# Group-norm statistics on ScalarE in place of VectorE, and one more product with C on VectorE in a quarter of layer 0's steps

## The chip, the cores and the metric

The kernel runs on one core of a Trainium2 chip. The metric is the device time of one execution in microseconds (us). The engines are called as the profile calls them: PE (TensorE, matmul), DVE (VectorE), ACT (ScalarE), POOL (GpSimd) and SP (SyncE, which issues all DMAs here). Each works through its own queue in order.

## What is computed

The input x is (8, 384, 32, 32) in float32: 8 batches, 384 channels, 1024 tokens. Four layers follow each other, each of the form x = x + f(gn(x)), where gn is a group norm over 32 groups of 12 channels and all 1024 tokens.

```python
def _gn(v, G=32, eps=1e-5):
    g = v.reshape(B_, G, C_ // G, H_, W_)
    m = jnp.mean(g, axis=(2, 3, 4), keepdims=True)
    s = jnp.var(g, axis=(2, 3, 4), keepdims=True)
    return ((g - m) / jnp.sqrt(s + eps)).reshape(v.shape)
...
def step(h, inp):                       # layers 0 and 2, over 1024 tokens
    dt_t, B_t, C_t, u_t = inp
    dA = jnp.exp(dt_t[..., None] * A)
    h = dA * h + (dt_t * u_t)[..., None] * B_t[:, None, :]
    y = jnp.einsum('bdn,bn->bd', h, C_t)
    return (h, y)
```

Layers 0 and 2 are Mamba blocks: a projection to 2 x 768 channels, a causal convolution of width 3, silu, a projection to dt, B and C, the recurrence above with 16 states for each of 768 channels, a gate silu(z), and a projection back to 384. Layer 2 has a layer norm ahead of it and an MLP (384 to 1536 to 384, gelu) behind. Layer 1 is a 1x1 projection, a filter in the Fourier domain of 8x8 patches, a depthwise 3x3 convolution, a gelu gate and a 1x1 projection. Layer 3 is a depthwise 3x3 convolution.

## The kernel before

**Tiling.** Each batch is cut into two chunks of T = 512 tokens. Layer 0 works through 16 chunks (numbers 0 to 15), layer 2 through 16 more (16 to 31). Layer 1 of a batch runs beside the later chunks of layer 0, layer 3 beside those of layer 2. Layer 1's result goes to HBM (x_mid) and comes back for layer 2.

**A step.** The recurrence of a chunk takes NQ = 24 steps. A step i has 32 channels x 16 states, held as four tiles of 128 partitions x 512 tokens, j = 0 to 3. For each step:
- begins: a DMA spreads dt*u from HBM into a tile g of 128 x 4 x 512 (5 buffers).
- times: POOL multiplies all of g by B (bc[:, 0], 2048 columns).
- decays: PE spreads dt into the four PSUM banks dA0 to dA3 (one buffer each).
- exps: ACT makes exp(A*dt) in place in each bank.
- scans: DVE runs the recurrence, tile by tile. For j below `low` the result goes into g, for the others into the bank dA.
- carries: in a batch's first chunk ACT copies the last column as the next chunk's start.
- states: POOL multiplies the tiles below `low` in g by C (bc[:, 1]).
- The other tiles are multiplied by C on DVE, out of the bank into g, right after the four scans.
- gathers: PE sums over the states into y; gatings: DVE multiplies y by the gate.

`low` is 4 minus the step's entry in SHARE. Before, every step has share 2: two tiles are multiplied by C on POOL in one operation of 1024 columns, two on DVE in two operations of 512. A decay for the next step waits until the bank's last reader is done: the scan for j below `low`, the product for the others.

**Statistics.** group_stats collects the mean and variance of each channel row (3 blocks of 512 columns for each of two halves), then two small matmuls with gmat average over the group. It is called once for each batch and layer, 32 times. For batches of layer 0 after the first, and for layer 2, `measure` loads 128 x 512 blocks from HBM through two xk buffers; for the first batch, layer 1 and layer 3 the blocks are already in SBUF. Before, each block is one bn_stats on DVE, and bn_aggr joins the six.

**Order.** The order of instructions on each queue is written by a planner when the kernel is built. Every piece of work is a generator; `yield on("ACT", ...)` names the engine of its next instruction and its operands. `Order.run` takes, again and again, the piece that could begin soonest by a table of costs (class Clocks), with the recurrence's processes first. Work beside the recurrence is spread by `pace`, and three PSUM banks (NBANK) are handed out by ps_take and ps_give. start_jobs adds the jobs of a chunk when its first step begins.

Of the kernel before, what the change touches and what calls it, by code (L numbers as in the profile page):

```python
# [9 lines left out]
F32 = mybir.dt.float32  # L10
# [6 lines left out]
P = 128  # L17
# [29 lines left out]
NBANK = 3  # L47
LEAD = 2
PATIENCE = 6.0
TAPS, LAST_TAPS = 4, 4  # L50
SHARE = (2, 2, 2, 2)
SET_EXP = "natural_log_exp_and_others"


# [195 lines left out]
def tile_conv_preact_d4(ctx: ExitStack, tc: tile.TileContext, a: dict, out: bass.AP):  # L250
# [179 lines left out]


    def group_stats(blocks, read=None):
        st = new(wk, [P, 2 * KC, 6], F32, "st", 2)
        mv = new(wk, [P, 2], F32, "mv", 2)
        for h, k, v, then in blocks():
            yield on("DVE", v)
            vector.bn_stats(st[:, h * KC + k, :], v)
            if then:
                yield from then()
        if read:  # L440
            read()
        yield on("DVE", st)
        vector.bn_aggr(mv, _flat(st))
        nmean, spread, rstd, nbias = (
            new(wk, [P, 1], F32, tag, 4) for tag in ("gnm", "gsp", "grstd", "gnb")
        )
        yield on("PE", mv, when=bank)
        ps, tag = ps_take("ps_gn")
        mm(ps[:, 0:1], gmat, mv[:, 0:1])
        yield on("ACT", ps)  # L450
        act(nmean, ps[:, 0:1], AF.Copy, scale=-1.0)
        ps_give(ps, tag)
        act(spread, mv[:, 0:1], AF.Square, bias=nmean)
        act(spread, spread, AF.Identity, bias=mv[:, 1:2])
        yield on("PE", spread, when=bank)
        ps, tag = ps_take("ps_gn")
        mm(ps[:, 0:1], gmat, spread)
        yield on("ACT", ps)
        rsqrt(rstd, ps[:, 0:1], eps_gn)
        ps_give(ps, tag)  # L460
        act(nbias, nmean, AF.Identity, scale=rstd)
        return rstd, nbias
# [2 lines left out]
        rstd, nbias = stats  # L465
        act(dst, src, AF.Identity, scale=rstd, bias=nbias)

    def measure_first():
        def blocks():
            for h in range(NCH):  # L470
                for k in range(KC):
                    yield h, k, first[h][:, k, :], None

        chunks[0]["stats"] = yield from group_stats(blocks)

    def measure(s):
        yield on(None, when=xk_free.when)
        xk_free.take()

        def load(h, k):  # L480
            x = new(wk, [P, T], F32, "xk", 2)
            sync.dma_start(x, _rows(s["src"][s["b"], :, h * T : (h + 1) * T])[:, k, :])
            return x

        places = [(h, k) for h in range(2) for k in range(KC)]
        loaded = []
        for h, k in places[:2]:
            yield on("SP")
            loaded.append(load(h, k))

        def blocks():
            for q, (h, k) in enumerate(places):

                def then():
                    if q + 2 < len(places):
                        yield on("SP")
                        loaded.append(load(*places[q + 2]))

                yield h, k, loaded[q], then

        s["stats"] = yield from group_stats(blocks, xk_free.give)

# [91 lines left out]
    def front(s):  # L594
# [23 lines left out]

        def block(d):
            if n not in (0, B * NCH - 1, B * NCH):  # L620
                yield pace(s["t"] - 18 + d)
            ps, tag = yield from projection(s, "ps_in", d * P)
            yield on("ACT", ps)
            act(u[d], ps, AF.Identity, scale=vec[:, d, 2:3], bias=vec[:, d, 3:4])
            if c < NCH - 1:
                act(s["xt"][:, d, :], ps[:, T - 2 : T], AF.Copy)
            for j in (1, 2):
                yield on("DVE", u[d])
                vector.scalar_tensor_tensor(
                    u[d][:, j:T], ps[:, 0 : T - j], vec[:, d, 2 - j : 3 - j],  # L630
                    u[d][:, j:T], ALU.mult, ALU.add,
                )
            ps_give(ps, tag)
# [35 lines left out]

        def step(d):  # L670
            if n not in (0, B * NCH - 1, B * NCH):
                yield pace(s["t"] - 9 + 3 * d)
# [12 lines left out]
            yield on("DVE", m, when=dt_free.when)  # L685
            dt_free.take()
            v = new(wk, [P, T], F32, "dt", 2)
            vector.scalar_tensor_tensor(v, ps, 0.0, m, ALU.max, ALU.add)
            ps_give(ps, tag)
            yield on("ACT", v, when=pc_free.when)  # L690
            pc_free.take()
            pc = new(wk, [P, NPC, T], BF16, "pc", 2)
            act(pc[:, 0, :], v, AF.Copy)
            if s["pre"] == "l0_":
                yield on("PE", pc[:, 0, :], when=bank)
                rest, tag = ps_take("ps_dr")
                mm(rest, eye, v, stop=False)
                mm(rest, minus, pc[:, 0, :], start=False)
                m_free.give()
            else:  # L700
                yield on("POOL", pc[:, 0, :])
                gpsimd.tensor_sub(m, v, pc[:, 0, :])
                rest, tag = m, None
            order.add(scaled(d, v), s["t"] - 14)
            yield on("ACT", rest)
            act(pc[:, 1, :], rest, AF.Copy)
            if tag:
                yield on("DVE", pc[:, 1, :])
# [32 lines left out]
    def seen(*keys):  # L741
# [4 lines left out]

        return ready

    def begins():
        for t, (s, i) in enumerate(steps):  # L750
            k, sub = QUADS[i]
# [30 lines left out]
    def decays():  # L782
        for t, (s, i) in enumerate(steps):
            k, sub = QUADS[i]
            for j in range(4):
                procs["decays"]["due"] = t - 2
                yield on("PE", when=lambda: (
                    None if ("begin", t) not in said or t > 0 and (
                        ("scan" if j < 4 - SHARE[(i - 1) % NSUB] else "product", t - 1, j) not in said
                        or j > 0 and not carried(t - 1, j)  # L790
                    )
                    else max(clocks.known(s["dts"][k]), clocks.last.get(dAs[j].name, 0.0))
                ))
                mm(dAs[j], selr[:, j, :], s["dts"][k][:, sub, :])
                said["decay", t, j] = True
# [9 lines left out]
    def scans():  # L805
        for t, (s, i) in enumerate(steps):
            for j in range(4):
# [2 lines left out]
                    else clocks.known(s["g", i][:, j, :])  # L810
                ))
                g = s["g", i]
                low = 4 - SHARE[i % NSUB]
                q = 4 * i + j
                vector.tensor_tensor_scan(
                    g[:, j, :] if j < low else dAs[j],
# [14 lines left out]
    def carries():  # L831
        for t, (s, i) in enumerate(steps):
            if s["c"] == NCH - 1:
                continue
            low = 4 - SHARE[i % NSUB]
# [11 lines left out]

    def carried(t, j):
        s, i = steps[t]
        low = 4 - SHARE[i % NSUB]  # L850
        return s["c"] == NCH - 1 or ("carry", t, j) in said or 0 < j < low

    def states():
        for t, (s, i) in enumerate(steps):
            low = 4 - SHARE[i % NSUB]
# [168 lines left out]
    def layer1(s):  # L1024
# [4 lines left out]
        def blocks():  # L1029
            for h in range(2):  # L1030
                for k in range(KC):
                    yield h, k, x[h][:, k, :], None

        gn = yield from group_stats(blocks)
        hurry = s["n"] == B * NCH - 1
        for hb in range(H // PS):
            if not hurry:
# [181 lines left out]
    def layer3(s):  # L1219
# [4 lines left out]
        def blocks():  # L1224
            for h in range(2):
                for k in range(KC):
                    yield h, k, x[h][:, k, :], None

        gn = yield from group_stats(blocks)
        taken = [0]  # L1230
        taps = TAPS if b < B - 1 else LAST_TAPS
        for k in range(KC):
# [47 lines left out]
    def start_jobs(t):  # L1280
# [2 lines left out]
            return  # L1283
        s = chunks[n]
        order.add(gates(s, 1), t + 8)
        if s["c"] == 0 and n + NCH < len(chunks):
            m = chunks[n + NCH]
            order.add(measured(m), t + NQ + 4)
        if n + 1 < len(chunks):
            later = chunks[n + 1]  # L1290
            order.add(front(later), t + NQ - 26)
# [177 lines left out]
```

## Time and profile before

| | |
|---|---|
| median of 3 runs | 6279.72 us (6264.88 to 6286.1) |
| the profiled execution, its own time | 6281.34 us |
| its span, first to last instruction | 6279.6 us |
| busy: PE, DVE, ACT, POOL | 5835.6, 5623.6, 4234.9, 5720.2 us |
| granted TensorE clock, mean | 0.965 |
| HBM traffic | 190 GB/s over the span |

A line of a group reads: source line, engine, operation, output tile <- input tiles, shapes, count, then busy time in us and mean ns of one, then the idle time of the engine just before and what ended it. Nearly all instructions carry line 189, that of a helper, so groups are told apart by tile names. A line of waits reads: who waited <- for whom: us in total, times, longest. In a table of stretches, each engine has its busy us and its count of instructions. PE's ends are modelled, so a busy PE is not PE at its peak.

### The profile page before, as it was taken

To read this page: it belongs to the slowest core of one execution; us is meant where nothing else is said; L and a number is where in the kernel's file an instruction comes from. 1 tells how busy PE (TensorE), PEld (TensorE's weight loads), DVE (VectorE), ACT (ScalarE), POOL (GpSimd) and SP (SyncE) were. 2 spreads that over 40 slices of the span, in tenths; PEclk is the share of its full clock that TensorE was granted. 3 is DMA by queue.
4 is the path that set the end of the run, shared out by engine and by line. 5 is a ranking of instruction groups with operands and counts; after the bars stand their busy time and mean duration, and the time that the engine had idled before them with its cause. 6 is when DMAs were issued, how large, how long until landed. Compare 5 with 4: busy or idle time off the path is not lost.

```text
span 6279.6 us, 62636 instructions
## 1 busy us (share of the span) xinstructions
PE 5835.6 (93%) x19010; PEld 2196.0 (35%) x19010; DVE 5623.6 (90%) x6392; ACT 4234.9 (67%) x7940; POOL 5720.2 (91%) x2022
## 2 busy tenths in 40 slices
PE   6878999999999999989989999999999999999997
PEld 2223333333333333333333333333333333333333
DVE  4999989999999989988887999999998999989992
ACT  4656677677767667766676766777677676667752
POOL 4999989999998999989997999999999999999980
PEclk8889999999999999999999999999999999999998
DMA  6877878887887878877777888888787787887871
GB/s 174 189 186 185 193 186 194 206 189 192 195 191 182 193 197 199 200 183 179 185 178 182 203 205 208 213 201 209 191 214 195 196 208 189 207 203 197 197 186 35
DMA packets 345860, 1195.88 MB, mean 190 GB/s; under 512 B 40420, under 2 KB 142484, under 8 KB 247220
## 3 DMA queue, kind: packets, MB, share of 16 engines
q1 hardware_dynamic: 345524, 1191.88, 78.0%
q8 instruction: 152, 2.49, 0.2%
q14 instruction: 184, 1.51, 0.1%
HBM read 1040.73 MB, written 150.99 MB: 190 GB/s over the span
## 4 chain that ended last, share of the span: by engine, by line
DVE 18%; PE 14%; POOL 12%; ACT 7%; issue 5%; DMA 3%; SPq 0%; DVEq 0%; POOLq 0%; ACTq 0%
POOL g L189 10%; DVE g L189 8%; DVE dA L189 5%; PE ps_up L189 3%; PE ps_dn L189 2%; PE y L189 2%; DMA g<-dud 2%; DVE ps_dw L189 2%; ACT dA L189 2%; PE dA L189 2%; DVE u L189 1%; PE ps_dw L189 1%; ACT h L189 1%; ACT L370 1%; ACT L189 1%
## 5 line engine op out<-in xcount | busy, mean ns | idle before, releaser
L189 POOL TENSOR_TENSOR g<-g,bc 128x1024 f32<-128x1024 f32 (+1 forms) x1536 | 5241.0, 3445 | 279.4 <-ACT carry L189 111.8
L189 ACT ACTIVATE dA<-dA,w_A 128x512 f32<-128x512 f32 x3072 | 2018.6, 661 | 964.1 <-PE dA L189 952.5
L189 PE MATMUL dA<-dts,selr 96*128 96x512 bf16 x3072 | 1193.7, 391 | 248.1 <-DVE g L189 223.7
L189 DVE TENSOR_TENSOR_SCAN g<-dA,carry,g 128x512 f32<-128x512 f32 x768 | 954.7, 1270 | 70.8 <-POOL g L189 55.2
L189 DVE TENSOR_TENSOR g<-dA,bc 128x512 f32<-128x512 f32 x1536 | 994.5, 678 | 20.4 <-ACT carry L189 18.8
L189 DVE TENSOR_TENSOR_SCAN dA<-dA,carry,g 128x512 f32<-128x512 f32 x768 | 953.8, 1273 | 42.6 <-ACT dA L189 42.1
L189 DVE TENSOR_TENSOR_SCAN dA<-dA,g 128x512 f32<-128x512 f32 x768 | 910.2, 1212 | 65.8 <-ACT dA L189 65.5
L189 DVE TENSOR_TENSOR_SCAN g<-dA,g 128x512 f32<-128x512 f32 x768 | 908.0, 1209 | 61.8 <-POOL g L189 43.9
L189 PE MATMUL y<-g,sely 128*32 128x512 f32 x6144 | 866.9, 632 | 47.0 <-POOL g L189 44.4
L189 PEld LDWEIGHTS <-selr 96*128 96x128 bf16 x3072 | 300.8, 99 | 1117.6 <-issue 1070.2
L189 PE MATMUL ps_in<-xf,w_in 128*128 128x512 f32 x1152 | 574.0, 619 | 3.7 <-ACT xf L189 3.3
L189 PE MATMUL ps_dn<-h,mw 128*128 128x512 f32 x1152 | 556.5, 605 | 13.9 <-ACT h L189 8.0
L189 PE MATMUL ps_z<-xf,w_in 128*128 128x512 f32 x1152 | 564.3, 596 | 4.0 <-DVE dt L189 3.6
L189 PE MATMUL ps_up<-t,mw 128*128 128x512 f32 x1152 | 556.9, 597 | 5.0 <-DVE acc L189 1.8
L189 PE MATMUL ps_out<-u,w_out 128*128 128x512 f32 x1152 | 552.0, 595 | 0.2 <-DVE x L189 0.2
L189 PE MATMUL ps_dw<-tp,diag 128*128 128x512 f32 x864 | 435.0, 606 | 8.9 <-ACT diag L189 8.8
L189 PEld LDWEIGHTS y<-g,sely 128*32 128x32 f32 x6144 | 127.6, 109 | 618.4 <-issue 296.1
L189 PEld LDWEIGHTS ps_dn<-h,mw 128*128 128x128 f32 x1152 | 218.8, 193 | 288.1 <-issue 245.5
L189 PEld LDWEIGHTS ps_in<-xf,w_in 128*128 128x128 f32 x1152 | 220.8, 197 | 273.8 <-issue 237.0
L189 POOL TENSOR_TENSOR dt<-dt,u 128x512 f32<-128x512 f32 x192 | 244.1, 1273 | 74.6 <-ACT pc L189 60.0
L189 PEld LDWEIGHTS ps_up<-t,mw 128*128 128x128 f32 x1152 | 215.6, 191 | 265.6 <-issue 227.5
L189 PEld LDWEIGHTS ps_z<-xf,w_in 128*128 128x128 f32 x1152 | 215.9, 190 | 253.2 <-issue 219.6
(112 smaller groups left out, 6471.2 us busy)
## 6 DMA issues: line engine op xcount, KB each, us to landing
g<-dud SPq DMA_DIRECT2D x768, 1024.0 KB, 7.8
dtd<-pc SPq DMA_DIRECT2D x192, 384.0 KB, 3.9
dts<-dtd SPq DMA_DIRECT2D x192, 384.0 KB, 7.8
mw<-in_l_mlp_w SPq DMA_DIRECT2D x192, 384.0 KB, 6.1
dud<-dt SPq DMA_DIRECT2D x768, 64.0 KB, 3.2
xf<-in_x SPq DMA_DIRECT2D x16, 768.0 KB, 9.2
x<-in_x SPq DMA_DIRECT2D x16, 768.0 KB, 11.4
x_mid<-x SPq DMA_DIRECT2D x16, 768.0 KB, 7.4
```

The source lines that it names most:

```text
L189: return call(out_, *args, **kw)
L370: nc.scalar.preload_act_table_set(SET_EXP)
```

## The change

There are three parts.

1. group_stats works on ACT in place of DVE. Each block is copied onto itself with a running sum along its columns (accum_out), and squared, less a shift, with another running sum. The shift is minus the mean of the first block, so that the squares stay small. Blocks loaded from HBM (junk is False) are squared in place. Chunks in SBUF are copied as one operation of 1536 columns, and squared in three of 512 into a PSUM bank whose content is not used. Five small ACT operations at the end give mean and variance.
2. SHARE is given for each layer. In layer 0 one step of four has share 3: one tile is multiplied by C on POOL, three on DVE. Layer 2 keeps share 2.
3. In layer 0 the statistics of a batch are asked for one chunk earlier, at the start of a batch's second chunk, three chunks ahead. In layer 2 they stay where they were. The small tiles of statistics get 6 buffers in place of 4.

```diff
-SHARE = (2, 2, 2, 2)
+SHARE = {"l0_": (2, 3, 2, 2), "l2_": (2, 2, 2, 2)}
...
     def group_stats(blocks, read=None):
-        st = new(wk, [P, 2 * KC, 6], F32, "st", 2)
-        mv = new(wk, [P, 2], F32, "mv", 2)
-        for h, k, v, then in blocks():
-            yield on("DVE", v)
-            vector.bn_stats(st[:, h * KC + k, :], v)
+        st = new(wk, [P, 2, 2 * KC], F32, "st", 2)
+        mv = new(wk, [P, 5], F32, "mv", 2)
+        shift, mean, off, sq, var = (mv[:, q : q + 1] for q in range(5))
+        count = 0
+        for v, junk, then in blocks():
+            columns = v.free_size()
+            yield on("ACT", v)
+            act(v, v, AF.Copy, accum_out=st[:, 0, count : count + 1])
+            if count == 0:
+                act(shift, st[:, 0, 0:1], AF.Copy, scale=-1.0 / columns)
+            if junk:
+                yield on("ACT", when=bank)
+                ps, tag = ps_take("ps_sq")
+                for k in range(KC):
+                    act(ps, v[:, k, :], AF.Square, bias=shift, accum_out=st[:, 1, KC * count + k : KC * count + k + 1])
+                ps_give(ps, tag)
+            else:
+                act(v, v, AF.Square, bias=shift, accum_out=st[:, 1, count : count + 1])
+            count += 1
             if then:
                 yield from then()
         if read:
             read()
-        yield on("DVE", st)
-        vector.bn_aggr(mv, _flat(st))
+        yield on("ACT", st)
+        act(st[:, 0, 0:count], st[:, 0, 0:count], AF.Copy, scale=1.0 / L / KC, accum_out=mean)
+        act(st[:, 1, :], st[:, 1, :], AF.Copy, scale=1.0 / L / KC, accum_out=var)
+        act(off, shift, AF.Identity, bias=mean)
+        act(sq, off, AF.Square)
+        act(var, sq, AF.Identity, scale=-1.0, bias=var)
...
-        yield on("PE", mv, when=bank)
+        yield on("PE", mean, when=bank)
         ps, tag = ps_take("ps_gn")
-        mm(ps[:, 0:1], gmat, mv[:, 0:1])
+        mm(ps[:, 0:1], gmat, mean)
...
-                yield h, k, loaded[q], then
+                yield loaded[q], False, then
...
+    def share(t):
+        s, i = steps[t]
+        return SHARE[s["pre"]][i % NSUB]
...
                 g = s["g", i]
-                low = 4 - SHARE[i % NSUB]
+                low = 4 - share(t)
...
-        gn = yield from group_stats(blocks)
+        gn = yield from group_stats(whole_chunks(x))
...
-        if s["c"] == 0 and n + NCH < len(chunks):
-            m = chunks[n + NCH]
-            order.add(measured(m), t + NQ + 4)
+        ahead_by = NCH + 1 if s["c"] == 1 and n + NCH < B * NCH else NCH
+        for m in chunks[n + NCH : n + NCH + 2]:
+            if m["c"] == 0 and "asked" not in m and m["n"] - n <= ahead_by:
+                m["asked"] = True
+                order.add(measured(m), t + NQ + 4)
```

The new whole_chunks yields x[0] and x[1], each whole, with junk set to True; measure_first, layer1 and layer3 use it. In scans, carries, carried, states and decays the step's share is read through share(t).

More of the change, by code (lines that the diff above doesn't have):

```diff
@@ L49 @@
 PATIENCE = 6.0
-TAPS, LAST_TAPS = 4, 4
-SHARE = (2, 2, 2, 2)
+TAPS, LAST_TAPS = 4,4
+SHARE = {"l0_": (2, 3, 2, 2), "l2_": (2, 2, 2, 2)}
 SET_EXP = "natural_log_exp_and_others"
@@ L441, in group_stats @@
             read()
-        yield on("DVE", st)
-        vector.bn_aggr(mv, _flat(st))
+        yield on("ACT", st)
[4 more added lines that the diff above has]
+        act(var, sq, AF.Identity, scale=-1.0, bias=var)
         nmean, spread, rstd, nbias = (
-            new(wk, [P, 1], F32, tag, 4) for tag in ("gnm", "gsp", "grstd", "gnb")
+            new(wk, [P, 1], F32, tag, 6) for tag in ("gnm", "gsp", "grstd", "gnb")
         )
-        yield on("PE", mv, when=bank)
+        yield on("PE", mean, when=bank)
         ps, tag = ps_take("ps_gn")
-        mm(ps[:, 0:1], gmat, mv[:, 0:1])
+        mm(ps[:, 0:1], gmat, mean)
         yield on("ACT", ps)
@@ L452, in group_stats @@
         ps_give(ps, tag)
-        act(spread, mv[:, 0:1], AF.Square, bias=nmean)
-        act(spread, spread, AF.Identity, bias=mv[:, 1:2])
+        act(spread, mean, AF.Square, bias=nmean)
+        act(spread, spread, AF.Identity, bias=var)
         yield on("PE", spread, when=bank)
@@ L466, in group_norm, with whole_chunks, measure_first @@
         act(dst, src, AF.Identity, scale=rstd, bias=nbias)
-    def measure_first():
+    def whole_chunks(x):
         def blocks():
             for h in range(NCH):
-                for k in range(KC):
-                    yield h, k, first[h][:, k, :], None
-        chunks[0]["stats"] = yield from group_stats(blocks)
+                yield x[h], True, None
+        return blocks
+    def measure_first():
+        chunks[0]["stats"] = yield from group_stats(whole_chunks(first))
     def measure(s):
@@ L620, in block @@
             if n not in (0, B * NCH - 1, B * NCH):
-                yield pace(s["t"] - 18 + d)
+                yield pace(s["t"] + -18 + 1 * d)
             ps, tag = yield from projection(s, "ps_in", d * P)
@@ L671, in step @@
             if n not in (0, B * NCH - 1, B * NCH):
-                yield pace(s["t"] - 9 + 3 * d)
+                yield pace(s["t"] + -9 + 3 * d)
             ps, tag = yield from chain(
@@ L788, in decays @@
                     None if ("begin", t) not in said or t > 0 and (
-                        ("scan" if j < 4 - SHARE[(i - 1) % NSUB] else "product", t - 1, j) not in said
+                        ("scan" if j < 4 - share(t - 1) else "product", t - 1, j) not in said
                         or j > 0 and not carried(t - 1, j)
@@ L834, in carries @@
                 continue
-            low = 4 - SHARE[i % NSUB]
+            low = 4 - share(t)
             yield on("ACT", when=lambda: (
@@ L849, in carried @@
         s, i = steps[t]
-        low = 4 - SHARE[i % NSUB]
+        low = 4 - share(t)
         return s["c"] == NCH - 1 or ("carry", t, j) in said or 0 < j < low
@@ L854, in states @@
         for t, (s, i) in enumerate(steps):
-            low = 4 - SHARE[i % NSUB]
+            low = 4 - share(t)
             procs["states"]["due"] = t + 0.3
@@ L1027, in layer1 @@
         yield once(lambda: "layer1" in said and (s["n"] < NCH or "done" in chunks[s["n"] - NCH]))
[L1029 to L1032, printed above, removed]
-        gn = yield from group_stats(blocks)
+        gn = yield from group_stats(whole_chunks(x))
         hurry = s["n"] == B * NCH - 1
@@ L1222, in layer3 @@
         yield once(lambda: s["n"] < (B + 1) * NCH or "done" in chunks[s["n"] - NCH])
[L1224 to L1229, printed above, removed]
+        gn = yield from group_stats(whole_chunks(x))
         taken = [0]
```

## Prediction

> **What bounds the kernel now.** I read the busy row of each engine first, then the same by stage, then the groups by shape, then who waits for whom.
>
> ```profile
> PE 5835.6 (93%) x19010; PEld 2196.0 (35%) x19010; DVE 5623.6 (90%) x6392; ACT 4234.9 (67%) x7940; POOL 5720.2 (91%) x2022
> 700.00:2500.00 1800.00, 1694.65 (x5798) 640.12 (x5797) 1686.32 (x1918) 1265.07 (x2527) 1721.83 (x575) 0.97 0.80 193
> 3200.00:5600.00 2400.00, 2317.23 (x7436) 876.02 (x7429) 2201.38 (x2486) 1684.86 (x2973) 2265.75 (x842) 0.99 0.81 200
> ```
>
> The two lower lines are the stages (columns: length, then busy of PE, weight loads, DVE, ACT, POOL). The first is steady layer 0 with layer 1 beside it, the second steady layer 2 with layer 3. Three engines are nearly level in both; only ACT has room (70%). POOL does 480 operations on g in the first stretch and 587 in the second, 48 to a chunk: 10.0 chunks of 180.0 us, and 12.2 of 196 us. Per chunk of layer 0 that is POOL 172.2 us (95.7%), PE 169.5 (94.2%), DVE 168.6 (93.7%), ACT 126.5 (70.3%); of layer 2, PE 189.5 (96.6%), POOL 185.3 (94.4%), DVE 180.0 (91.7%), ACT 137.8 (70.2%). So POOL is fullest in layer 0, and PE in layer 2.
>
> The groups by shape give the prices:
>
> ```profile
> L189 POOL TENSOR_TENSOR g<-g,bc 128x2048 f32<-128x2048 f32 x768 | 3478.2, 4533 | 107.9 <-DMA g<-dud 98.8 <-PE dA L189 2.3 <-PE ps_dt L189 2.0
> L189 POOL TENSOR_TENSOR g<-g,bc 128x1024 f32<-128x1024 f32 x768 | 1808.9, 2357 | 171.5 <-ACT carry L189 111.8 <-DVE g L189 57.9 <-PE dA L189 0.3
> L189 DVE TENSOR_TENSOR g<-dA,bc 128x512 f32<-128x512 f32 x1536 | 994.5, 678 | 20.4 <-ACT carry L189 18.8
> L189 DVE BATCH_NORM_STATS2 st<-xk 128x6 f32<-128x512 f32 x90 | 60.8, 676 | 0.2 <-DMA xk<-x_mid 0.2
> L189 DVE BATCH_NORM_AGGREGATE mv<-st 128x2 f32<-128x36 f32 x32 | 9.6, 300 | 0.1
> L189 ACT ACTIVATE u<-u 128x1536 f32<-128x1536 f32 x64 | 91.5, 1476 | 0.4
> L189 ACT ACTIVATE sq<-xf 128x512 f32<-128x512 f32 x48 | 30.0, 625 | 13.8 <-DVE xf L189 13.8
> L189 ACT ACTIVATE gsp<-mv,gnm 128x1 f32<-128x1 f32 x32 | 9.4, 295 | 1.2 <-ACT gnm L189 0.2
> ```
>
> See that a statistic on DVE costs what a product with C costs there (676 and 678 ns), so the two can be exchanged one for one; and that POOL's 1024-wide product waits most for ACT's carry copies.
>
> The waits of steady layer 0, DVE's and then POOL's:
>
> ```profile
> DVE u L189 <- PE y L189: 36.5, 28, 2.6
> DVE dA L189 <- ACT dA L189: 21.5, 17, 2.4
> DVE x L189 <- PE ps_out L189: 18.4, 5, 3.9
> ...
> POOL g L189 <- ACT carry L189: 33.5, 16, 4.1
> POOL g L189 <- DMA g<-dud: 30.5, 13, 5.1
> ```
>
> DVE's largest wait is for y, which PE can gather only after POOL's product: POOL holds DVE up there. The next on both engines is for ACT, the engine that is to get the new work.
>
> **What the Trainium skill says.** "ScalarE: Activation LUTs", section "What ACT_TABLE_LOAD costs": each pointer operand adds about 93 ns to an ACTIVATE. The trace agrees: h<-ps_up with one pointer takes 687 ns, t<-ps_out without one 595. "Perfetto Trace Analysis", section "Identifying the Most-Contended Engine", says that matmul busy time is no measure of distance to PE's limit; this trace shows 94% in layer 0 and 96.6% in layer 2 on that row, so PE's row has at least that much left in layer 0. "GPSIMD Engine Reference", section "Elementwise — side-by-side cycle accounting", has 4497 ns for a 2048-wide two-input operation on POOL and 2293 on DVE; here POOL takes 4533.
>
> **The change part by part.**
>
> *Products with C.* Where the share is 3, POOL multiplies 512 columns in place of 1024. From the two POOL rows the slope is (4533-2357)/1024 = 2.125 ns a column, so 512 columns take 1269 ns (dt<-dt,u, 512 wide, shows 1273). Saved: 1088 ns in 16 chunks x 6 steps = 96 places, 104 us of POOL, 6.5 us a chunk of layer 0. DVE makes one more product there: 96 x 678 = 65 us, 4.07 us a chunk. POOL's product can also begin one scan (some 1.2 us) earlier, since only one state must be scanned. Against that the decay bank dA1 comes free only after its product: two products and a scan (1.3 + 1.2 us) still lie over PE's 0.39 and ACT's 0.66 us for the next decay, so I cost it at nothing; if ACT is late there, it becomes a DVE wait. ACT copies one carry more in half of these places: 48 x 174 ns = 8 us.
>
> *Statistics leave DVE.* 192 x 676 ns and 32 x 300 ns, 139 us. Per chunk 6 x 676 + 300 = 4.36 us.
>
> *Statistics on ACT.* For a batch measured from memory: six in-place Copies of 512 columns (633 as pc<-dt) and six Squares with a pointer (625 + 92): 8.1 us. For a batch measured in place: two Copies of 1536 (1476) and six Squares: 7.3 us. The end of each: a shift of 0.17, two short sums at 0.2, three one-column operations at 0.295: 1.45 us. The running sum is not in the trace. It may come with the ACTIVATE (0), or need a read of its own, at most one of the one-column operations (0.3); I take 0.2, for 14 and 10 sums. So 12.35 and 10.75 us. There are 15 of the first (7 in layer 0, 8 in layer 2) and 17 of the second (the first batch, 8 in layer 1, 8 in layer 3): 368 us (290 to 410). A chunk gets half of one of each, 11.5 us: ACT goes from 70% to 77% in layer 0 and 76% in layer 2. Behind a block on ACT's queue stand exponentials, PSUM evictions and carries: 1.4 us a block from memory, 3.6 us in place, with exponentials let in between Copy and Squares.
>
> *Squares into a PSUM bank.* 34 times some 2.8 us, 95 us of one bank in three over the span: nothing while another is free; at worst a chain of matmuls waits as long.
>
> *Asked for a chunk earlier in layer 0.* The same 90 loads on SP's queue, 0.35 us each to issue; six pass other transfers by a chunk. They land in a median of 5.4 us, and the statistics were not waited for in steady layer 0. Nothing; if they push g's loads back, POOL's 30 us of waits for g show it (0 to 10 us).
>
> *The ends, which nothing covers.* At the start x has landed when DVE begins at 10.76 us, and its aggregate ends at 14.7; PE's first projection (20.1) waits for ACT's norm. ACT's 10.75 us from about 10 end near 20.8: +6. At the end the first half's sums fit into ACT's idle 21 us before gnm; after the last addition (6221.3) remain one Copy, three Squares, the sums' reads and the end: 1.48 + 2.15 + 1.2 + 1.45 = 6.3 against DVE's 3.9: +2.
>
> **The sum.** In layer 0 POOL falls to 165.7 us a chunk and DVE stays (168.6 + 4.07 - 4.36 = 168.3), so DVE and PE are the fullest. If DVE can be as full as POOL is now, 95.7%, a chunk takes 175.9 us (-4.1); if it stays at 93.7%, 179.6 (-0.4). I take the middle, -2.25, because ACT's extra 11.5 us works against the better end: 16 x -2.25 = -36. In layer 2 DVE's 4.36 us are free time on the third fullest engine; PE keeps 96.6%. I take 0 (-30 to +30). With the ends, -36 + 8 = -28. The profiled execution took 6281.3 (span 6279.6), 1.6 over the median of 6279.7: **6253**.
>
> **The rivals.** (1) *No arrival*: DVE, not POOL, sets layer 0's pace. For it: DVE is 3.6 us a chunk behind POOL. Against: its largest wait is on POOL's product. Then -0.4 x 16 + 8: 6283, no change; 0.25. (2) *ACT late, slower*: blocks of sums stand before exponentials and carries. DVE's waits on ACT (exponentials 127, carries 19, spm 34 us) and POOL's (carry 112, pc some 31 without the start) come to 320 us. ACT's free share falls from 30% to 23.5%; if waits grow as its inverse, by 1.28, that is 90 us, and two thirds of it on the path 60: -28 + 60, 6313. It decides once ACT's waits grow the path by over 47 us. For it: both engines' waits on ACT; against: ACT itself idles 950 us for PE's decays. 0.28. (3) *Full relief*: 16 x -4.1, and half of layer 2's 16 x 4.36, with the ends: -66 - 30 + 8, 6193; 0.12. (4) *Nothing of the share is done*, as the order is planned with other costs for sums: the count of 512-wide POOL products would be 0, not 96. Hardly possible; in (1).
>
> **How the numbers follow.** Forecast 0.35, (3) 0.12: faster by over 0.3% 0.47; (1): same 0.25; (2): slower 0.28. 0.3% (19 us) is about what a measurement of this kernel can tell from no change. The likeliest case alone runs from 6215 to 6262; the range reaches to (3) and past (2): 6190 to 6325.
>
> **What would show it.** No BATCH_NORM rows; 96 POOL products of 512 at 1.27 us and 672 of 1024; 1632 DVE products; ACT near 4600 us; layer 0's chunk at 177 to 178 us and layer 2's still at 196; u<-y waits shrunk. Wrong if layer 0's pace holds at 180 with POOL at 92% (rival 1), or if DVE's waits for ACT's dA and POOL's for carry grow by more than a third (rival 2), or if layer 2's pace moves by over 2 us.

## The result, and the profile after

The changed kernel takes 6298.91 us (median of 9 runs, 6290.65 to 6306.67), the kernel before 6276.08 (9 runs on the same chips): a ratio of 1.0037, 95% interval 1.0027 to 1.0048. It is slower by some 23 us, where 6253 and faster was forecast. Its profiled execution took 6294.31 us (span 6292.2), 13 over the one of before. The medians differ by 23, so stretches of these two single executions are to be read to within some 10 us.

The busy row of the page:

```profile
PE 5811.4 (92%) x19010; PEld 2191.1 (35%) x19010; DVE 5564.7 (88%) x6264; ACT 4515.0 (72%) x8876; POOL 5618.9 (89%) x2022
```

DVE lost 59 us, POOL 101, PE kept its work; ACT gained 280. No busy engine explains a longer run, so the loss is in waits. The groups of the new work, by shape:

```profile
L189 POOL TENSOR_TENSOR g<-g,bc 128x512 f32<-128x512 f32 x96 | 122.3, 1274 | 4.9 <-DVE g L189 4.2 <-ACT carry L189 0.7
L189 DVE TENSOR_TENSOR g<-dA,bc 128x512 f32<-128x512 f32 x1632 | 1052.7, 678 | 16.9 <-ACT carry L189 15.3
L189 ACT ACTIVATE ps_sq<-x,mv 128x512 f32<-128x512 f32 x96 | 66.6, 694 | 7.2 <-DVE x L189 4.4 <-DVE u L189 0.6
L189 ACT ACTIVATE xk<-xk,mv 128x512 f32<-128x512 f32 x90 | 65.0, 722 | 2.9
L189 ACT ACTIVATION_READ_ACCUMULATOR xk<-xk,mv 128x1 f32 x90 | 16.8, 186 | 0.0
```

The prices were right: 1274 ns for POOL's 512 columns (1269 forecast), 694 and 722 for a Square (717), and a running sum has a read of its own, here 186 ns (0.2 us). What the sum of busy times can't tell is where it went. So I cut the span at the first POOL product with B of a chunk, found by counting the 768 of them: at the start of chunk 17 and of chunk 31. Chunk 17 is early in layer 2, and layer 1's last batch has then mostly gone by. Before, then after (columns as in the table of stretches):

```profile
0.00:3185.36 3185.36, 2879.27 (x9652) 1074.09 (x9653) 2876.19 (x3273) 2159.42 (x4290) 2953.02 (x1002) 0.95 0.79 190
3185.36:5922.71 2737.35, 2644.84 (x8499) 998.50 (x8497) 2524.19 (x2855) 1923.51 (x3408) 2590.60 (x963) 0.99 0.81 200
5922.71:6279.60 356.89, 311.51 (x864) 123.40 (x860) 223.21 (x266) 151.93 (x244) 176.54 (x59) 0.93 0.48 123
```

```profile
0.00:3151.52 3151.52, 2844.48 (x9644) 1067.91 (x9645) 2866.32 (x3243) 2316.75 (x4836) 2851.45 (x1002) 0.95 0.80 192
3151.52:5922.55 2771.03, 2644.73 (x8484) 996.79 (x8483) 2478.70 (x2767) 2022.63 (x3738) 2587.53 (x960) 0.99 0.80 197
5922.55:6292.20 369.65, 322.15 (x885) 126.43 (x882) 219.70 (x256) 175.59 (x303) 179.94 (x61) 0.93 0.48 123
```

Read the first number after the colon pair, the length. To chunk 17 the change gains 34 us. From 17 to 31 it loses 34, with PE's and POOL's busy time the same to within 4 us and DVE 45 us lighter. The last stretch loses 13. The granted TensorE clock (the third number from the right: 0.95, 0.99, 0.93) is the same before and after. The gain to chunk 17 is near the forecast of layer 0 with its start (-36 + 6 = -30), though at the start of chunk 16, where layer 0 ends, it is only 19; the loss of layer 2 was forecast as 0.

The waits of that middle stretch, before:

```profile
POOL g L189 <- ACT carry L189: 41.4, 26, 4.5
POOL g L189 <- DVE g L189: 34.5, 19, 5.5
POOL spm L189 <- ACT pc L189: 31.1, 15, 9.1
...
DVE dA L189 <- ACT dA L189: 60.5, 37, 4.3
DVE g L189 <- POOL g L189: 55.3, 36, 4.4
```

and after:

```profile
POOL g L189 <- ACT carry L189: 64.7, 32, 5.3
POOL spm L189 <- ACT pc L189: 43.0, 18, 9.8
POOL g L189 <- DVE g L189: 37.0, 16, 6.8
...
DVE g L189 <- POOL g L189: 70.6, 43, 5.0
DVE dA L189 <- ACT dA L189: 70.5, 40, 3.7
```

POOL waits 35 us more for ACT (carry and pc, the latter part of making dt), and DVE 15 more for POOL and 10 for ACT. No wait for a statistic by name comes to 3 us in total.

Where in a chunk do these waits fall? Call the time from a chunk's last product with B to the next chunk's first one its hand-over. The 14 hand-overs from chunk 17 to 31 take 191 us before and 227 after; all the rest takes 2547 and 2544. The hand-over of chunk 24 to 25 has the largest difference, before and then after:

```profile
4726.03:4747.93 21.90, 21.30 (x70) 7.79 (x70) 18.57 (x21) 20.09 (x39) 19.71 (x12) 1.00 0.62 175
4705.85:4746.99 41.14, 38.54 (x118) 14.27 (x117) 26.68 (x32) 31.11 (x58) 24.36 (x15) 0.96 0.37 107
```

POOL (the fifth busy time) is idle for 2 us of it before and for 17 after, waiting for carry and pc. Over all, POOL's idle time grows by 21 us in the hand-overs and by 16 elsewhere, while 15 us of its work, 11 of them on the next chunk's dt, have moved into the hand-overs. So the lost time shows where a chunk ends and the next one is not ready; the steps keep their length, with less other work among them and more waiting.

### The profile page after: what moved, and what is told of

It reads as the page before. It is cut to its first block, busy times and chain, and to the rows that moved or that the text cites. A ratio compares the mean times of both kernels' runs of the same rounds, so it can differ in the third digit from the quotient of the medians.

```text
span 6292.2 us, 63467 instructions
## 1 busy us (share of the span) xinstructions
PE 5811.4 (92%) x19010; PEld 2191.1 (35%) x19010; DVE 5564.7 (88%) x6264; ACT 4515.0 (72%) x8876; POOL 5618.9 (89%) x2022
## 3 DMA queue, kind: packets, MB, share of 16 engines
q14 instruction: 191, 1.56, 0.1%
## 5 line engine op out<-in xcount | busy, mean ns | idle before, releaser
L189 POOL TENSOR_TENSOR g<-g,bc 128x1024 f32<-128x1024 f32 (+2 forms) x1536 | 5139.3, 3378 | 358.8 <-ACT carry L189 127.6
L189 DVE TENSOR_TENSOR g<-dA,bc 128x512 f32<-128x512 f32 x1632 | 1052.7, 678 | 16.9 <-ACT carry L189 15.3
L189 DVE TENSOR_TENSOR_SCAN dA<-dA,carry,g 128x512 f32<-128x512 f32 x816 | 1012.0, 1273 | 61.2 <-ACT dA L189 60.5
L189 DVE TENSOR_TENSOR_SCAN dA<-dA,g 128x512 f32<-128x512 f32 x816 | 964.8, 1213 | 96.7 <-ACT dA L189 95.6
L189 DVE TENSOR_TENSOR_SCAN g<-dA,carry,g 128x512 f32<-128x512 f32 x720 | 895.6, 1270 | 83.0 <-POOL g L189 68.5
L189 DVE TENSOR_TENSOR_SCAN g<-dA,g 128x512 f32<-128x512 f32 x720 | 850.7, 1209 | 77.0 <-POOL g L189 39.6
L189 PE MATMUL y<-g,sely 128*32 128x512 f32 x6144 | 862.0, 628 | 48.5 <-POOL g L189 45.5
```

The lines of the kernel that those rows point to most:

```text
L189: return call(out_, *args, **kw)
```

## The experiments

Two theories stood at the start. *Theory 1*: the moves do this by themselves, POOL's relief gaining in layer 0 and ACT's sums losing in layer 2. *Theory 2*: the order of the queues is written by a greedy planner, any change makes it write another, and another order of the same work moves the time by as much. Reading the whole set is easiest in one table: start of chunk 17, length from 17 to 31, the rest (profiled execution, us), and the median of the timed runs with its ratio to runs of the kernel before that were made beside them.

| kernel | to 17 | 17 to 31 | rest | median | ratio (95%) |
|---|---|---|---|---|---|
| before | 3185 | 2737 | 357 | 6276 | |
| nudge (before, 0.101) | 3214 | 2741 | 355 | 6315 | 1.0067 (1.0053-1.0080) |
| before_099 | 3169 | 2738 | 357 | 6266 | 0.9989 (0.9982-0.9996) |
| before_102 | 3220 | 2742 | 355 | 6314 | 1.0058 (1.0042-1.0075) |
| the change | 3152 | 2771 | 369 | 6299 | 1.0037 (1.0027-1.0048) |
| after_099 | 3160 | 2780 | 359 | 6304 | 1.0044 (1.0029-1.0059) |
| after_101 | 3169 | 2799 | 358 | 6326 | 1.0074 (1.0059-1.0089) |
| after_102 | 3167 | 2781 | 360 | 6319 | 1.0064 (1.0049-1.0079) |
| after_aware | 3157 | 2756 | 361 | 6278 | 1.0009 (1.0000-1.0017) |
| share_only | 3191 | 2737 | 365 | 6288 | 1.0024 (1.0017-1.0031) |
| stats_only | 3153 | 2788 | 365 | 6308 | 1.0055 (1.0041-1.0068) |
| act_early | 3178 | 2777 | 361 | 6312 | 1.0062 (1.0049-1.0075) |
| act_early_099 | 3161 | 2729 | 364 | 6254 | 0.9969 (0.9958-0.9981) |
| act_late | 3156 | 2787 | 369 | 6312 | 1.0061 (1.0046-1.0076) |
| ask_only | 3159 | 2735 | 362 | 6261 | 0.9973 (0.9962-0.9984) |
| ask_101 | 3165 | 2744 | 354 | 6264 | 0.9981 (0.9970-0.9992) |
| plan_stats | 3252 | 2795 | 353 | 6401 | 1.0200 (1.0185-1.0215) |
| plan_share | 3243 | 2738 | 357 | 6338 | 1.0103 (1.0087-1.0118) |
| plan_both | 3303 | 2796 | 354 | 6455 | 1.0286 (1.0270-1.0301) |
| plan_none | 3167 | 2736 | 348 | 6253 | 0.9968 (0.9956-0.9979) |

### Parts of the change, and a control

share_only is the kernel before with the new SHARE; stats_only the change with the old one; act_early the change with the statistics of layers 2 and 3 back on DVE. nudge changes one of the planner's costs and no work:

```diff
-    SAME, OTHER = 0.034, 0.1
+    SAME, OTHER = 0.034, 0.101
```

> The kernel before with only the share (2, 3, 2, 2) in layer 0; all statistics stay on VectorE. Theory 1 (the freed POOL time is the gain in layer 0, and ACT's sums cost time in layer 2): layer 0 loses 6.5 us of POOL a chunk but DVE goes from 168.6 to 172.7 us, so DVE gets as full as POOL was; layer 0 gains little, 0 to -15 us at the start of chunk 16, and layer 2 stays: 6262 to 6280 us. Theory 2 (a new plan moves the time by itself, whatever the change): anything between 6255 and 6300, with layer 2's pace moved although nothing in layer 2 was changed. If the share alone gives the whole gain of layer 0 (-20 to -30 us), DVE was not full.

> The changed kernel with share 2 everywhere: all statistics on ACT, nothing moved from POOL to DVE. Theory 1: layer 0 is set by POOL, which keeps its 172 us a chunk, so the start of chunk 16 stays within 10 us of before or gets later by up to 15 us; layer 2 loses the same 35 us and the tail 12 us: 6310 to 6335 us. Theory 2: the loss in layer 2 is no property of the sums, and this other plan shows a loss of another size there, from -15 to +50 us.

> The changed kernel with the statistics of layers 2 and 3 back on VectorE (bn_stats and bn_aggr as before); first batch, layer 0 and layer 1 keep the sums on ACT, and layer 0 keeps share 3 in one step of four. Theory 1: chunk 17 begins some 30 us earlier than before, as in the changed kernel, and from there the pace is that of before, the tail too: 6276 - 30 = 6246 us, 6238 to 6256. Theory 2: layer 2 is planned anew all the same, so its length may differ from before by up to 30 us either way: 6220 to 6280.

> The kernel before with one number of the planner's costs changed, the delay between engines from 0.100 to 0.101 us: the same work, planned in another order. Theory 1 needs this to be small beside the effect: within 12 us of before. Theory 2 expects a difference as large as that of the change, 20 us or more either way.

The control is the finding: the same work in another order takes 6315 us. The share alone left chunk 17 where it was (+6) although POOL has 104 us less to do there; stats_only, with POOL's work as before, gained 32. That speaks against POOL's relief as the gain of layer 0, the first step of theory 1. Theory 2 missed too in one point: share_only kept layer 2 at 2737 us. act_early, with layer 2's work as before, lost 39 us there.

What a plan does can be a single event. Of nudge's 28 us at chunk 17 all stand in one hand-over, of chunk 9 to 10, which takes 36.5 us in place of 6.8 (before_102, below, has the same one); of act_early's 39 us 38 stand in that of chunk 22 to 23 (48.5 in place of 10.2). So single plans can't be compared to within 20 us. The next runs hold the order.

### The order held, the work moved

Here the planner is told the old costs, so every choice comes out as before, and the moved work is put in without its knowledge. PE's and SP's queues keep their order to the instruction. For the statistics (clocks.op books the old cost; raw issues an activation that the planner does not see; where x is still needed, `to` is a dead part of a convolution's input tile; in-place batches are copied in six blocks, not two; lines on the shift and on the blocks from memory are left out):

```diff
             yield on("DVE", v)
-            vector.bn_stats(st[:, h * KC + k, :], v)
+            clocks.op("DVE", "bn_stats", st_d[:, q, :], [v])
+            raw(v, v, AF.Copy, accum_out=st[:, 0, q : q + 1])
...
+                raw(to, _img(v), AF.Square, bias=shift, accum_out=st[:, 1, q : q + 1])
```

For the share, in one step of four of layer 0, tile 1 is scanned into its bank and multiplied at once. (The change itself multiplies after all four scans, so this is not quite its move.) In a batch's first chunk ACT makes a carry copy for it on the spot:

```diff
+                if three:
+                    if s["c"] < NCH - 1:
+                        nc.scalar.activation(carry[:, q : q + 1], dAs[j][:, T - 1 : T], AF.Copy)
+                    nc.vector.tensor_mul(g[:, j, :], dAs[j], s["bc"][:, 1, :])
```

> The statistics alone moved from DVE to ACT (two sums for each block of 512 columns, six blocks each time), share 2 everywhere, and the order of every queue held as the kernel before has it: the planner is told the old costs, and the sums stand in ACT's queue where the bn_stats were issued; nothing is asked for earlier. PE, POOL and SP keep their order to the instruction. Theory 1 (the sums make ACT late, above all in layer 2): layer 0 gains 10 to 25 us from DVE's 4.4 us a chunk, layer 2 loses 20 to 40 us with POOL's waits for carry grown by a third or more, the ends lose 10: 6275 to 6305 us. Theory 2 (the loss is that of a new plan, not of the sums): both layers gain or keep their time, the ends lose 8 us: 6245 to 6278.

> The share alone: in one step of four of layer 0, DVE makes the product of a third tile right after its scan (ahead of the other two scans), ACT takes that tile's carry from the bank, POOL multiplies 512 columns in place of 1024; statistics as before, and the order of all other instructions held as before. Theory 1 (POOL sets layer 0's pace): layer 0 gains 20 to 35 us, 6240 to 6255. The other reading (DVE sets it, as the run of the share alone and the run of the statistics alone let one think): DVE is 4.07 us a chunk fuller and layer 0 loses up to 30 us: 6275 to 6300 us.

> Both moves with the order held as before. Theory 1: the sum of the two, about -25 in layer 0, +30 in layer 2, +10 at the ends: 6280 to 6300 us. Theory 2: without a new plan both moves do what the prediction said: layer 0 25 to 40 us shorter, layer 2 within 15 us, ends +8: 6240 to 6265 us.

Both moves lose, by far more than expected: 121 us and 59 us of span, together 173. Theory 2 in its plain form (the moves are good, the new plan is bad) is false. It is the other way round: the moves are bad where they stand, and planning anew, together with the earlier asking that these runs lack, wins most of that back. Where the sums act shows in POOL's and DVE's waits of plan_stats to chunk 17:

```profile
POOL g L189 <- ACT carry L189: 113.2, 43, 7.3
...
DVE dA L189 <- ACT dA L189: 77.6, 38, 4.4
...
DVE g L189 <- ACT carry L189: 48.0, 52, 2.8
```

Before, over the same work, these three were:

```profile
POOL g L189 <- ACT carry L189: 70.3, 33, 4.9
...
DVE dA L189 <- ACT dA L189: 44.5, 31, 3.3
...
DVE g L189 <- ACT carry L189: 16.4, 25, 1.6
```

108 us more of waiting for ACT, for 66 us of time. With the order held, rival 2 of the prediction is right. But this is not the changed kernel's loss of layer 2: from chunk 17 to 31 plan_stats keeps the hand-overs at 191 us, and the rest goes from 2547 to 2604.

plan_none leaves five of six bn_stats out and puts nothing in their place:

```diff
-            vector.bn_stats(st[:, h * KC + k, :], v)
+            if h == k == 0:
+                vector.bn_stats(st[:, 0, :], v)
+            else:
+                clocks.op("DVE", "bn_stats", st[:, h * KC + k, :], [v])
```

> The kernel before with the order of every queue held, and five of six bn_stats of each statistic left out (the first block alone stands for the mean and variance): 160 x 0.68 = 108 us of DVE taken away, nothing put on ACT. If DVE sets the pace of layer 0 (as one more product there, 65 us of DVE, cost 58 us with the order held), layer 0 gains 40 to 55 us; in layer 2, where PE is fullest, 0 to 25 us; the end 3: 6205 to 6235 us. If DVE does not set it, the gain is under 15 us: 6260 to 6275.

It gained 28 us of span, between the two forecasts. To chunk 17 DVE's busy time fell by 51 us and the time by 18; from 17 to 31 DVE lost 32 us and the time 1.5; the end gained 8.5. So a statistic on DVE was mostly filler: a third of its time counted in layer 0, a twentieth in layer 2. (That the statistics fall into gaps between the steps is a reading of these numbers.) With five of six blocks gone and nothing in exchange, the gain with this order is 28 us; plan_stats, which pays for the move on ACT, takes 149 us more than plan_none.

The extra product of plan_share looks like the opposite, 65 us more of DVE for 58 us of time, but the chunks tell another story. In layer 0 the two chunks of a batch differ. Chunks 8 and 9 (first and second of a batch) before, then in plan_share:

```profile
1510.07:1700.24 190.17, 174.30 (x602) 66.00 (x603) 174.00 (x205) 137.16 (x294) 176.65 (x63) 0.95 0.79 187
1700.24:1869.30 169.06, 164.42 (x559) 61.98 (x557) 163.78 (x181) 116.05 (x212) 168.42 (x54) 0.99 0.83 201
1544.24:1741.46 197.22, 176.30 (x609) 66.78 (x608) 181.34 (x215) 139.86 (x303) 170.34 (x64) 0.96 0.77 183
1741.46:1910.07 168.61, 162.98 (x554) 61.24 (x553) 164.52 (x183) 115.14 (x210) 162.07 (x55) 0.99 0.83 198
```

From chunk 4 to 14 the first chunks grow from 190.9 to 197.4 us in the mean; the second ones keep their 169 us, with the same product moved in both. In a second chunk POOL was 99.6% busy before; relieved of 6 us it gives nothing, as DVE (97%) and PE (97%) are next. In a first chunk no engine was over 93% busy, so there was no full engine to relieve, and the moved product waits 48 times, in every first chunk's six places, for the carry copy that the edit put into ACT's queue:

```profile
DVE g L833 <- ACT carry L832: 17.2, 48, 2.9
```

So the 58 us are not the price of DVE's product alone; how much of them is the copy's, no run separates.

### Several plans of each kernel

before_099, before_102, after_099, after_101 and after_102 differ from their kernels by the planner's delay alone, as the nudge does.

> The kernel before, planned with a delay between engines of 0.099 us in place of 0.100. Theory 2: a new plan of the same work is slower than this one, which is a lucky draw: 6290 to 6320 us, as with 0.101 (6315). If 0.101 was a chance of its own, 6265 to 6285 us.

> The changed kernel, planned with 0.099 us between engines. If a plan is a draw with a spread of some 25 us (before: 6273 with 0.100, 6266 with 0.099, 6315 with 0.101), the changed kernel's draws spread as widely around a centre of their own. Reading A (the change as such is worth nothing, 6299 was a poor draw): the mean over 0.099 to 0.102 is within 15 us of the mean of before. Reading B (the sums cost some 20 us even when planned for): the mean is 15 to 35 us over that of before. This one: 6270 to 6320 us.

> The changed kernel, planned with 0.101 us. The same readings; if the planner's number acted the same way on both kernels this would be 40 us slower than with 0.100, near 6340; if the draws are independent, 6260 to 6330 us.

> The changed kernel, planned with 0.102 us. As with 0.099: 6260 to 6330 us; A: mean of the four within 15 us of that of before; B: 15 to 35 us over it.

> The kernel before, planned with 0.102 us: the fourth draw of the old work, 6260 to 6320 us. Reading A wants the mean of its four near 6290 or above, B near 6275.

Four plans of the old work take 6276, 6266, 6315 and 6314 us, mean 6293; four of the new 6299, 6304, 6326 and 6319, mean 6312. The mean is 19 us higher, inside B; but the spread of the plans (standard deviations 25 and 13 us) leaves 14 us of uncertainty on that, so A is not excluded. The stretches tell more. To chunk 17 the new plans lie at 3152 to 3169, the old at 3169 to 3220: 35 us better in the mean (some 20 without the one bad hand-over of nudge and before_102). From 17 to 31 the new take 2771 to 2799, the old 2737 to 2742: 43 us worse. The two hardly touch in the first and are clear of each other in the second. So the change has a gain and a loss, and neither is one plan's chance.

### What the loss and the gain are

Three readings of the loss were left. *S*: the sums themselves cost time in layer 2. *U*: the planner counts a sum without its read, and so plans too tightly. *P*: it is a poor plan, which other work can draw as well. act_early_099 repeats act_early in another plan. act_late puts the sums into layers 2 and 3 alone, with share 2. after_aware lets the planner count a sum's read:

```diff
             self._clocks.op(self._name, what, out_, ins)
+            if "accum_out" in kw:
+                self._clocks.free[self._name] += 0.2
```

> Sums on ACT for the first batch, layer 0 and layer 1, share 3 in layer 0, old statistics in layers 2 and 3; planned with 0.099 us. S and U: chunk 17 begins 10 to 30 us early and layer 2 takes its 2737 us (to within 10): 6245 to 6268 us. P: layer 2 takes 20 to 50 us more, as with 0.100: 6280 to 6320 us.

> Sums on ACT in layers 2 and 3 alone, old statistics in layers 0 and 1, share 2 everywhere. S: from chunk 17 to 31 35 to 60 us longer than before, layer 0 like the old work's draws (-17 to +35 at chunk 17): 6295 to 6360 us. P: the same could come out, but not in every plan.

> The changed kernel, with 0.2 us more in the planner's cost of each running sum, what the profile shows its read to take. U: the loss from chunk 17 to 31 falls from 34 to 62 us to under 15, and the kernel takes 6245 to 6275 us. S and P: the loss stays over 25 us: 6285 to 6325 us.

With the sums in layers 2 and 3, seven plans take 2756 to 2799 us from chunk 17 to 31. Without, nine plans (four of before, share_only, two of act_early, two of ask_only) take 2729 to 2744 in eight cases and 2777 in one, act_early. So having the sums there costs time (S), some 40 us, and a poor plan can cost as much without them (P has one instance). In replanned kernels the difference lies in the hand-overs: 194 to 259 us in the seven plans, 177 to 198 in the eight and 246 in act_early, while the rest takes 2533 to 2562 with the sums and 2531 to 2566 without. Why plans with sums hand over later is not shown. after_aware has the lowest of the seven, a loss of 19 us (U had under 15, S and P over 25), with hand-overs of 194 us, and it is 4 us over the kernel before (1.0009). The planner's cost is likely part of the loss (U), but one plan does not settle that.

act_late gave the surprise: chunk 17 at 3156, with neither sums nor third product in layers 0 and 1. Up to there it shares with the change only the third part: statistics asked for a chunk earlier, with 6 buffers for the small tiles. (The edit also reaches the first batch of layer 2, whose statistics load in chunk 13 in place of 14.) ask_only and ask_101 are before and nudge with that part alone, buffers included:

```diff
-        if s["c"] == 0 and n + NCH < len(chunks):
-            m = chunks[n + NCH]
-            order.add(measured(m), t + NQ + 4)
+        ahead_by = NCH + 1 if s["c"] == 1 and n + NCH < B * NCH else NCH
+        for m in chunks[n + NCH : n + NCH + 2]:
...
```

> The kernel before with the third part of the change alone: in layer 0 the statistics of a batch, on DVE as before, are asked for one chunk earlier (and the small tiles of statistics have 6 buffers). If this part is the gain of layer 0: chunk 17 begins 15 to 35 us early, layer 2 keeps 2737 us, 6240 to 6260 us. If it is worth nothing: chunk 17 within the old work's draws, -17 to +35 us, and as likely late as early.

> The same, planned with 0.101 us, where the old work without this part began chunk 17 28 us late (6315 us). If this part is the gain: 15 to 35 us early again, 6240 to 6260 us. If not: some 20 to 35 us late, 6295 to 6320 us, or any other draw.

Both gain: chunk 17 at 3159 and 3165, where the same planner costs gave 3185 and 3214 (30 of nudge's us being its one hand-over). By medians the gain is 15 us over before and 51 over nudge. That is the gain of layer 0, asking and buffers not told apart. All eight plans with sums or share and the early asking lie around the same place (3152 to 3178, mean 3162), so sums and share add nothing visible to it. Layer 2 keeps its time, and both kernels are faster than before and than the change.

Why it gains is only partly seen. Before, the statistics of layers 0 and 1 stand in the first chunks of the batches: 12 bn_stats in each from chunk 2 to 14, none in the second ones. In ask_only each chunk has 6. Its chunks 8 and 9, to be held against those of before above:

```profile
1501.07:1683.03 181.96, 165.83 (x590) 64.22 (x589) 171.75 (x201) 134.59 (x288) 175.57 (x64) 0.97 0.80 193
1683.03:1857.57 174.54, 170.26 (x572) 64.83 (x572) 164.90 (x185) 120.62 (x219) 169.67 (x54) 0.98 0.81 197
```

The first chunks, which had room on every engine, become 8 us shorter (190.9 to 182.5 in the mean of chunks 4 to 14), the second 5 us longer (169.1 to 174.0). The statistics' last operation on ACT (gnb), in the two batches from 1500 to 1990 us, before and in ask_only:

```profile
L189 ACT ACTIVATE gnb<-gnm,grstd x4: 295/296/296, 1611.8 to 1973.4; 128x1 f32<-128x1 f32 x4
L189 ACT ACTIVATE gnb<-gnm,grstd x4: 294/294/294, 1522.2 to 1956.1; 128x1 f32<-128x1 f32 x4
```

Before, the measured batch's and layer 1's statistics of a batch end together (the four at 1612, 1614, 1971 and 1973 us); with early asking they are 78 us apart (1522, 1600, 1877, 1956). DVE's wait for y in steady layer 0, shown with the prediction at 36.5 us, is then 2.5; to chunk 17 it falls from

```profile
DVE u L189 <- PE y L189: 60.4, 44, 4.0
```

to

```profile
DVE u L189 <- PE y L189: 20.5, 18, 3.6
```

But this wait is not the gain: DVE's waits for ACT's dA and POOL's g rise at the same time, from 44.5 and 39.4 us to 64.8 and 64.5. That two bursts apart disturb the recurrence less than two at once is argued, not shown: no run moved the asking to other places.

## Why the prediction was wrong

**What held.** Every price of an instruction, the counts, ACT's new load (the rows of the sums, their reads and the small operations add up to 361 us, with 368 forecast; the busy row rises by 280 only, since neighbours on ACT overlap; in the steady stretch of layer 0 ACT is at 75.5%, with 77% forecast). Of the signs that were to show it wrong, one appeared in full, layer 2's pace moved by 2.4 us a chunk, and one in part: POOL's waits for carry grew by more than a third in layer 2 only. (A slip in rival 3: half of 16 x 4.36 is 35, not 30; it bears on nothing here.)

**The first step that failed: "16 x -2.25 = -36".** The number nearly came out (-34 at chunk 17, -19 at chunk 16), by luck: the reason was another. It was built on POOL being fullest in layer 0 and on DVE's relief. With the order held, taking the product off POOL and onto DVE cost 59 us; planned anew without the early asking (share_only) it gave +6. The 95.7% was a mean of two kinds of chunk: in the second ones POOL was 99.6% busy and set the pace, with PE and DVE at 97%, so that relieving it gave nothing; in the first it was 92.5% busy and set no pace. Nor did POOL's product hold DVE up through y: in ask_only that wait all but vanished with POOL's work unchanged.

**The second: "asked for a chunk earlier ... Nothing".** It is worth 26 us at chunk 17 in one plan and 49 in the other, some 30 of the 49 being one hand-over. I looked only at whether the loads would be late, and not at where the statistics fall among the other work.

**The third, which decides the sign: "In layer 2 DVE's 4.36 us are free time ... I take 0".** The relief is indeed worth nothing (plan_none: 1.5 us). But I then let ACT's 11.5 us a chunk be nothing too, though I had put the same load against the better end in layer 0. Layer 2 lost 34 us in this plan and 34 to 62 in the four, 2.4 to 4.4 us for each of 14 chunks; act_late, with the sums in layers 2 and 3 alone, lost 49. Rival 2 named the waits and scaled them by 1.28; in layer 2 POOL's wait for carry grew by 1.56, and in layer 0 with the order held by 1.6 (carry), 1.7 (dA) and 2.9 (carry on DVE). What neither the forecast nor rival 2 had is a term for the hand-over between chunks, where the changed kernel's 34 us lie (191 to 227 us). That bursts of sums on ACT make the next chunk's dt late there is argued; no run moved the sums within a chunk.

**The ends.** +8 was forecast. The start cost 1.5 us (chunk 0 at 73.5 against 72.1), not 6. ACT, which has nothing else to do, began when x landed at 5.97 us:

```profile
5.97 1.48 ACT L189 ACTIVATE xf<-xf 128x1536 f32<-128x1536 f32 x1 [3.95 <-DMA xf<-in_x]
```

DVE's 10.76 us, from which I had reckoned, came after earlier work of DVE, which waits for another load until 9.83 us; it was not the landing of x. At the end, from the last addition to the end of the statistics, 5.3 us took the place of 3.9 (+2 forecast). The 13 us of the last stretch lie between the start of chunk 31 and that addition, and the other plans of the change show 2 to 5 in that stretch, share_only without any sums 8: most likely a matter of the plan.

**The Trainium skill** held where it was used: 93 ns for a pointer ("ScalarE: Activation LUTs", section "What ACT_TABLE_LOAD costs") is seen again in Square on the xk tiles, 722 ns against 625 for the layer norm's without a pointer. That PE's matmul busy time is no measure of its limit ("Perfetto Trace Analysis", section "Identifying the Most-Contended Engine") is not contradicted: in layer 2 that row stayed at 2645 us while the length grew by 34. How far PE is from its limit, no run here shows.

**The size of the question.** The order of the queues moves this kernel by up to 50 us with no work changed. A forecast of -28 from a sum of parts lay within what a new plan does by itself, and the prediction had no term for that.

## What to carry to other kernels

Where the order is written by a planner, measure a few plans of the same work first (change a cost by 1%); a difference smaller than their spread can't be put down to the edit from one plan of each. To see what a move itself costs, hold the order and let the planner believe in the old one; to see what it could gain, leave the work out. Read such runs by stretch, and within a stretch by what repeats: here first and second chunks, steps and hand-overs behaved differently, which the busy share of the whole layer hid. And price a moved instruction by where it stands: 51 us of statistics between the steps counted for 18, and as sums on ACT, with the order held, the same statistics cost more time than leaving them out could gain.

## What was not expected of the hardware

A running sum on ACT is two instructions in these traces: the ACTIVATE, and an ACTIVATION_READ_ACCUMULATOR of 186 to 201 ns. In the start of the changed kernel a Square of 512 columns with its read takes 0.85 us, from the start of one Square (7.81 us) to that of the next (8.66). The ACTIVATE itself is not slower for it: 1481 ns for 1536 columns copied with a sum, 1476 for silu on as many without one.
